# Two attention blocks on one core: the first couple's bounds-check passes over its reciprocals, issued 4 and 6 units later

## The chip, the cores and the metric

The kernel runs on one core of a Trainium2 chip. The metric is the device time of one execution in microseconds; lower is better. Before the change the median of nine runs is 2905.37 us (2904.89 to 2906.02). Tensors are float32 throughout.

## The reference, cut to what matters

Eight samples of 512 channels and 32 x 32 positions pass through two attention layers, each with a residual. The change lies in the first layer, which has 8 heads of 64 channels:

```python
h = group_norm(x, norm_w, norm_b)
qkv = jnp.einsum('oc,bchw->bohw', qkv_w, h) + qkv_b[None, :, None, None]
qkv = qkv.reshape(B, 3, nh, hd, N).transpose(1, 0, 2, 4, 3)
q, k, v = (qkv[0], qkv[1], qkv[2])
attn = jnp.einsum('bhnd,bhmd->bhnm', q, k) * scale
attn = jax.nn.softmax(attn, axis=-1)
o = jnp.einsum('bhnm,bhmd->bhnd', attn, v)
o = o.transpose(0, 1, 3, 2).reshape(B, C, H, W)
o = jnp.einsum('oc,bchw->bohw', proj_w, o) + proj_b[None, :, None, None]
return x + o
```

The second layer is the same with one head of 512 channels and a norm over the whole sample.

## The kernel before, in words

The program is unrolled over the eight samples. For each, `layer0` makes the values, then runs the attention of layer 0, then projects; `attention1` does the second layer. Dense products use a Strassen-like scheme with seven products of quarters in place of eight; that part is away from the change.

**Softmax without a maximum.** The kernel takes exponentials of the raw scores (`exponentials`, L645), multiplies them with the values, and divides the result by the sum of the exponentials. That is right as long as nothing overflows, so the kernel checks bounds: the function `held` (L650 to L654) passes every sum and every reciprocal through ScalarE with the identity function and adds it up along the row into one column of a small tile `extent`. The passed values go to a tile `held` that nobody reads, or, for the sums of a couple, to the tile of the reciprocals-to-be. At the end of the kernel all columns of `extent` are compared with 1e15, and if one is too large, or not a number, a second, slower program with maxima runs. Nothing else reads `extent`.

**Units of attention.** The 8 heads make 4 pairs, taken in the order 0, 2, 1, 3. Each pair has two groups of 512 queries and 8 tiles of keys. One unit is one pair, one group and one tile of keys; 64 units make a sample. The loop at L899 runs over i and issues, in this order: the scores of unit i (L716, TensorE, into a PSUM tile `s`, of which there are two), their exponential (L645, ScalarE) with the sum of exponentials so far (L647, VectorE, `acc`), then the values of unit i - 2 (L735, TensorE, into `ps_o`). When a group of queries is done (after its eighth tile of keys), ScalarE copies one half of `ps_o` out (L741) and VectorE adds the other (L742). Last in each step comes `couple_steps(i)`, in all samples but the eighth, which divides in another way.

**Dividing by couples.** The pairs 0 and 2 make the first couple, 1 and 3 the second. The sums of a couple are finished together, in two parts g = 0 and 1, one for each group of queries. `couple_steps` counts units from the end of the couple's second pair, which for the first couple is unit 31:

- `fold` and `folded` bring together, by DMA and one addition, what the two groups' accumulators hold (1 and 5 steps behind).
- `sum_couple` adds over the partitions by matmuls with ones, into `ps_sum` (7 behind, i = 38).
- `copy_couple` passes part g of the sums through `held` (the bounds check on the sums), out of PSUM into the tile `inv` (7 and 8 behind).
- `one_over_couple` takes the reciprocal of `inv` in place on VectorE (L856) and issues eight DMAs that spread it over the partitions (8 and 10 behind).
- `held_couple` passes the reciprocals through `held` (the bounds check on the reciprocals; L867 to L868). The four numbers in the loop at L888 are the distances of copy, reciprocal, this pass and the division.
- `divide_couple` multiplies the outputs by the spread reciprocals on VectorE (L755; 13 and 15 behind).

The second couple ends with the loop; its steps hang on the q and k products of the next sample (L932 to L945) and go by numbers of their own.

**Order of the work.** The program is written with a manual schedule for TensorE, ScalarE and VectorE: each executes its instructions in the order in which the Python code issues them. The order of DMAs on SyncE is made by a planner. A tile is a buffer from a pool (36 for the large ones, two for `inv`, one for `held`); it comes free after its last reader, and a writer of the next tile in it waits for that.

Of the kernel before, what the change touches and what calls it, by code (L numbers as in the profile page):

```python
# [65 lines left out]
def two_attention_blocks(  # L66
# [31 lines left out]
    def banks(tag, name):  # L98
        return psum.tile([P, 2, HALF], FP, tag=tag, name=name)
# [590 lines left out]
    def layer0(bs, qs, ks, b, norm_next):  # L690
# [133 lines left out]
        def fold(pair):  # L824


            (a, c), t = (accs[pair, g] for g in range(2)), tile2(f"fold_{b}_{pair}")
            low, high = slice(0, HD), slice(HD, P)
            nc.sync.dma_start(t[low], a[high])
            nc.sync.dma_start(t[high], c[low])  # L830
            nc.sync.dma_start(a[high], c[high])
            folds[pair] = t

        def folded(pair):
            a = accs[pair, 0]
            nc.vector.tensor_tensor(a, a, folds.pop(pair), ALU.add)

        def sum_couple(couple, banks_of):


            for n, (pair, j) in enumerate((pair, j) for pair in couple for j in range(2)):
                for g, bank in enumerate(banks_of):
                    rows = slice(g * HD, (g + 1) * HD)
                    nc.tensor.matmul(  # L844
                        bank[n * 32 : (n + 1) * 32, :], ones[rows, :32], accs[pair, 0][rows, j, :],
                        start=True, stop=True,
                    )
            ps_couple[:] = banks_of

        def copy_couple(couple, g):  # L850
            name = f"{b}_{couple[0]}_{g}"
            invs[g] = accpool.tile([P, HALF], FP, tag="inv", name=f"inv_{name}")
            held(ps_couple[g], f"sum_{name}", invs[g])

        def one_over_couple(couple, g):
            nc.vector.reciprocal(invs[g], invs[g])  # L856
            for n, pair in enumerate(couple):
                if g == 0:
                    spreads[pair] = tile2(f"inv_{b}_{pair}")
                for j in range(2):  # L860
                    for r in range(2):
                        nc.sync.dma_start(
                            spreads[pair][(j * 2 + r) * 32 : (j * 2 + r + 1) * 32, g, :],
                            invs[g][(n * 2 + j) * 32 : (n * 2 + j + 1) * 32, :],
                        )

        def held_couple(g):  # L867
            held(invs.pop(g), f"inv_{b}_{g}")  # L868

        def divide_couple(couple, g):  # L870
            for pair in couple:
                divide(pair, g, spreads[pair][:, g, :])

        def ended(i):

            pair, g, kt = units[i] if 0 <= i < len(units) else (None, None, None)
            return pair if (g, kt) == (1, NT - 1) else None

        def couple_steps(i):
            if ended(i - 1) is not None:  # L880
                fold(ended(i - 1))
            if ended(i - 5) is not None:
                folded(ended(i - 5))
            couple = couples[0]
            if ended(i - 7) == couple[1]:
                ps_sum = banks("o", f"ps_sum_{b}_{couple[0]}")
                sum_couple(couple, [ps_sum[:, g, :] for g in range(2)])
            for g, (at_copy, at_over, at_held, at_divide) in enumerate([(7, 8, 10, 13), (8, 10, 12, 15)]):  # L888
                if ended(i - at_copy) == couple[1]:
                    copy_couple(couple, g)  # L890
                if ended(i - at_over) == couple[1]:
                    one_over_couple(couple, g)
                if ended(i - at_held) == couple[1]:
                    held_couple(g)
                if ended(i - at_divide) == couple[1]:
                    divide_couple(couple, g)

        last = norm_next is None
        for i in range(2, len(units) + 2):  # L899
            if i < len(units):  # L900
                score(i)
            values(*units[i - 2], ps.pop(i - 2))
            if not last:
                couple_steps(i)
                continue
            pair, g, kt = units[i - 5] if i >= 5 else (None, None, None)
            name = f"0_{b}_{pair}_{g}"
            if kt == NT - 1 and pair == end:
                ps_sum = banks("o", f"ps_sum_{name}")[:, 0, :]
                add_keys(pair, [g], ps_sum)  # L910
                held(ps_sum, f"sum_{name}")
                invs[pair] = one_over(ps_sum, name)
                divide(pair, g, invs[pair])
            elif kt == NT - 1 and g == 1:
                sum_both(pair, banks("o", f"ps_sum_{name}")[:, 0, :], name)
            pair, g, kt = units[i - 9] if i >= 9 else (None, None, None)
            if pair in invs and kt == NT - 1:
                held(invs.pop(pair), f"inv_0_{b}_{pair}_{g}")
            pair, g, kt = units[i - 10] if i >= 10 else (None, None, None)
            if pair in spreads and (g, kt) == (1, NT - 1):  # L920
                divide_both(pair)
# [809 lines left out]
```

## Time and profile before

| | |
|---|---|
| median of nine runs | 2905.37 us (2904.89 to 2906.02) |
| profiled execution | 2904.69 us, span 2903.0 us, TensorE clock 1.0 |
| TensorE | 2887.8 us busy (99%) |
| VectorE | 1756.5 us (61%) |
| ScalarE | 1090.9 us (38%) |
| `held` over reciprocals or others into the `held` tile (L654) | 41 passes, 630 ns (median) |
| reciprocals of couples (L856) | 28, 3344 ns (median) |
| exponentials (L645) | 512, 1024 ns mean |

The busy times are sums over the one profiled execution. Matmul ends are modelled, so consecutive matmul groups overlap a little in the lists; the distance from start to start is the firmer measure. In a row of waits, the first name is who waited, the second for whom, followed by the total, the number and the longest wait in us. A square bracket at the end of a line of a timeline gives the idle time of the engine just before, and what ended it.

### The profile page before, as it was taken

The numbers are of one execution on the slowest core, as the hardware profiler recorded it, in microseconds if no ns is written. First come the engines' busy times: TensorE is split into PE (matmuls) and PEld (weight loads), VectorE is DVE, ScalarE is ACT, GpSimd is POOL, SyncE is SP. The second block draws the span as 40 slices with busy tenths as digits, with TensorE's granted clock in tenths as the row PEclk, the third lists the DMA queues.
The fourth block names the chain that finished last, engine by engine and source line by source line (L and its number), as shares of the span: only waits on it lengthen the run. The fifth ranks groups of instructions, "written<-read, shape, count | busy, mean of one in ns | idle before, by whom it ended". The sixth has DMA issues, their size and how long they took to land.

```text
span 2903.0 us, 34605 instructions
## 1 busy us (share of the span) xinstructions
PE 2887.8 (99%) x14096; PEld 1363.4 (47%) x14096; DVE 1756.5 (61%) x2196; ACT 1090.9 (38%) x1520; POOL 21.0 (1%) x28
## 2 busy tenths in 40 slices
PE   9999999999999999999999999999999999999999
PEld 6434554345533455335553354533545335453354
DVE  5676366763667536676366753577545775537836
ACT  3462314623155231552315523165222642226431
POOL 0000000000000000000000000000000000000000
PEclk9999999999999999999999999999999999999999
DMA  8412122121222203212032121321212222112001
GB/s 271 158 41 73 51 95 91 41 73 51 94 93 46 84 33 110 79 44 91 26 120 75 41 90 32 113 77 45 83 54 91 77 55 81 54 57 68 8 1 38
DMA packets 77655, 210.79 MB, mean 73 GB/s; under 512 B 19888, under 2 KB 20656, under 8 KB 71088
## 3 DMA queue, kind: packets, MB, share of 16 engines
q1 hardware_dynamic: 77344, 208.48, 22.6%
q8 instruction: 112, 1.84, 0.3%
q14 instruction: 55, 0.45, 0.0%
q10 hardware_dynamic: 144, 0.02, 0.0%
HBM read 137.43 MB, written 28.57 MB: 57 GB/s over the span
## 4 chain that ended last, share of the span: by engine, by line
PE 96%; DVE 3%; ACT 1%; issue 0%; POOL 0%; ACTq 0%; DVEq 0%; POOLq 0%
PE s L716 14%; PE ps_o L735 14%; PE ps_q L479 13%; PE ps_v L494 13%; PE ps_s L1071 13%; PE ps_o L1129 13%; PE ps_k L479 7%; PE ps_p L479 6%; DVE inv L856 2%; DVE acc L647 1%; ACT p L645 1%; PE ps_wvo L596 0%; PE ps_wqk L626 0%; PE ps_o L1140 0%; PE ps_sum L844 0%
## 5 line engine op out<-in xcount | busy, mean ns | idle before, releaser
L645 ACT ACTIVATE p<-s 128x1024 f32<-128x1024 f32 x512 | 521.8, 1024 | 311.4 <-PE s L716 299.9
L716 PE MATMUL s<-q,k 64*64 64x512 f32 x4096 | 531.8, 591 | 8.2 <-ACT p L645 8.2
L647 DVE TENSOR_TENSOR acc<-acc,p 128x1024 f32<-128x1024 f32 x384 | 469.2, 1222 | 107.1 <-ACT p L645 96.7
L735 PE MATMUL ps_o<-p,v 64*64 64x512 f32 x4096 | 528.6, 589 | 0.0
L716 PEld LDWEIGHTS s<-q,k 64*64 64x64 f32 x4096 | 153.2, 133 | 299.4 <-issue 260.3
L735 PEld LDWEIGHTS ps_o<-p,v 64*64 64x64 f32 x4096 | 156.6, 133 | 282.9 <-issue 280.0
L1079 DVE TENSOR_TENSOR p<-ps_s,u_s 128x512 f32<-128x512 f32 x96 | 66.4, 692 | 246.9 <-ACT u_s L421 141.0
L528 DVE TENSOR_TENSOR v<-ps_v,u_v 128x512 f32<-128x512 f32 x96 | 66.2, 690 | 197.5 <-PE ps_v L494 126.2
L421 ACT COPY u_v<-ps_v 128x512 f32<-128x512 f32 x96 | 56.2, 585 | 305.8 <-PE ps_v L494 293.2
L1071 PE MATMUL ps_s<-s_q,t 128*128 128x512 f32 x384 | 167.4, 592 | 0.0
L1129 PE MATMUL ps_o<-t_p,s_v 128*128 128x512 f32 x384 | 166.1, 592 | 0.0
L421 ACT COPY u_q<-ps_q 128x512 f32<-128x512 f32 x96 | 55.8, 581 | 250.4 <-PE ps_q L479 250.4
L647 DVE TENSOR_TENSOR acc<-p,p 128x1024 f32<-128x1024 f32 x64 | 77.9, 1217 | 91.1 <-ACT p L645 91.1
L1081 ACT ACTIVATE p<-p,factor 128x512 f32<-128x512 f32 x96 | 69.3, 722 | 133.2 <-DVE p L1079 133.2
L1071 PEld LDWEIGHTS ps_s<-s_q,t 128*128 128x128 f32 x384 | 73.0, 190 | 91.8 <-issue 91.8
L1129 PEld LDWEIGHTS ps_o<-t_p,s_v 128*128 128x128 f32 x384 | 73.0, 190 | 91.8 <-issue 87.5
L479 PE MATMUL ps_q<-t,w_wqk 128*128 128x512 f32 x256 | 116.0, 597 | 0.0
L479 PE MATMUL ps_p<-t_p,w_p 128*128 128x512 f32 x256 | 114.3, 595 | 0.6 <-DVE inv L658 0.5
L1129 PE MATMUL ps_o<-p,v 128*128 128x512 f32 x256 | 113.3, 595 | 0.0
L494 PE MATMUL ps_v<-w_wvo,t 128*128 128x256 f32 x512 | 113.1, 379 | 0.0
L1071 PE MATMUL ps_s<-q,x 128*128 128x512 f32 x256 | 112.5, 592 | 0.0
L856 DVE RECIPROCAL inv<-inv 128x512 f32<-128x512 f32 x28 | 93.7, 3346 | 22.9 <-ACT inv L654 22.9
(261 smaller groups left out, 3605.8 us busy)
## 6 DMA issues: line engine op xcount, KB each, us to landing
x<-in_x SPq DMA_DIRECT2D x92, 512.0 KB, 7.0
w_qk<-stored_qk SPq DMA_DIRECT2D x14, 1792.0 KB, 7.3
inv<-inv SPq DMA_DIRECT2D x248, 64.0 KB, 2.0
w_wqk<-stored_wqk SPq DMA_DIRECT2D x8, 1792.0 KB, 7.6
fold<-acc SPq DMA_DIRECT2D x56, 256.0 KB, 3.1
w_wvo<-stored_wvo SPq DMA_DIRECT2D x8, 1792.0 KB, 7.8
out<-x SPq DMA_DIRECT2D x28, 512.0 KB, 2.8
w_v<-stored_v SPq DMA_DIRECT2D x7, 1792.0 KB, 7.1
```

The costliest lines, as they stand in the source:

```text
L421: nc.scalar.copy(us[n][:, :width], line[:, :width])
L479: nc.tensor.matmul(bank, w[a][:, k, c * P : (c + 1) * P], bs[b][:, k, :], start=fresh and k == 0, stop=k == 1, skip_group_check=True,)
L494: nc.tensor.matmul(bank[:, u * 2 * P : (u + 1) * 2 * P], bs[b][:, k, n * P : (n + 1) * P], w[a][:, k, :], start=fresh and u == k == 0, sto ...
L645: nc.scalar.activation(p, s, AF.Exp, scale=factor)
L647: nc.vector.tensor_tensor(acc, first, p, ALU.add)
L716: nc.tensor.matmul(s[cols, j, :], flat(ks[pair])[rows, k0 : k0 + HD], qs[pair][rows, g, :], start=True, stop=True,)
L735: nc.tensor.matmul(o[cols, half, :], vs[kt][rows, c0 : c0 + HD], p[rows, j, :], start=kt == 0, stop=kt == NT - 1,)
L856: nc.vector.reciprocal(invs[g], invs[g])
L1071: nc.tensor.matmul(bank, bs[b][:, k, t * P : (t + 1) * P], q_parts[a][:, k, :], start=fresh and k == 0, stop=k == 1, skip_group_check=True,)
L1079: nc.vector.tensor_tensor(p, bank, u, ALU.add)
L1081: nc.scalar.activation(p, bank, AF.Exp, scale=norm.factor)
L1129: nc.tensor.matmul(bank, v_parts[kt // 2][a][:, kt % 2, c * P : (c + 1) * P], p_parts[kt // 2][b][:, kt % 2, cols], start=fresh and kt == ...
```

## The change

In the loop over the two parts of a couple, the third distance, that of `held_couple`, goes from 10 to 14 for g = 0 and from 12 to 18 for g = 1. So the pass over the first part's reciprocals is issued at i = 45 and no longer at i = 41, and that over the second part's at i = 49 and no longer at i = 43. The passes themselves, what they read and what they add into `extent` are the same, and the divisions keep their places (i = 44 and 46), so that both passes now follow them.

```diff
@@ -885,7 +885,7 @@
             if ended(i - 7) == couple[1]:
                 ps_sum = banks("o", f"ps_sum_{b}_{couple[0]}")
                 sum_couple(couple, [ps_sum[:, g, :] for g in range(2)])
-            for g, (at_copy, at_over, at_held, at_divide) in enumerate([(7, 8, 10, 13), (8, 10, 12, 15)]):
+            for g, (at_copy, at_over, at_held, at_divide) in enumerate([(7, 8, 14, 13), (8, 10, 18, 15)]):
                 if ended(i - at_copy) == couple[1]:
                     copy_couple(couple, g)
                 if ended(i - at_over) == couple[1]:
```

## The prediction

> **What bounds the kernel now.** I read the head of the page first, then the whole list of TensorE's waits, which is three rows long.
>
> ```profile
> span 2903.0 us, 34605 instructions
> PE 2887.8 (99%) x14096; PEld 1363.4 (47%) x14096; DVE 1756.5 (61%) x2196; ACT 1090.9 (38%) x1520; POOL 21.0 (1%) x28
> ```
>
> The waits, with their total, number and longest:
>
> ```profile
> PE s L716 <- ACT p L645: 8.2, 7, 1.2
> PE ps_warm L1235 <- POOL in_sample L163: 1.2, 1, 1.2
> PE ps_p L479 <- DVE inv L658: 0.5, 1, 0.5
> ```
>
> TensorE sets the time: it works for 2887.8 of 2903.0 us, and all that it waits for other engines is 9.9 us. Of that, 8.2 us are seven equal stalls of 1.17 us, scores waiting for an exponential. An edit pays or costs here only if it touches those seven stalls or makes new ones. Seven is also the number of samples that run the changed function (all but the last of eight).
>
> Next I read the chain that ended last, around the first stall (start, length, what):
>
> ```profile
> 179.43 3.26 DVE inv L856
> ...
> 184.29 3.35 DVE inv L856
> 187.64 0.02 issue
> 187.66 0.02 ACTq L654
> 187.68 0.04 issue
> 187.72 0.07 ACT held_inv L654
> ...
> 188.26 0.18 ACT held_inv L654
> 188.44 0.92 ACT p L645
> 189.37 0.04 issue
> 189.41 1.09 PE s L716 x8
> ```
>
> At each stall the chain leaves TensorE: the couple's second reciprocal on VectorE ends at 187.64, ScalarE's pass over it (held_inv, L654) starts at 187.72, and only then come an exponential and the scores that need its PSUM bank. The timelines of TensorE and of ScalarE there, start and length in us:
>
> ```profile
> 186.35 1.04 PE L716 MATMUL s<-q,k 64*64 64x512 f32 x8
> 187.21 1.04 PE L735 MATMUL ps_o<-p,v 64*64 64x512 f32 x8
> 189.41 1.09 PE L716 MATMUL s<-q,k 64*64 64x512 f32 x8 [1.17 <-ACT p L645]
> 190.32 1.04 PE L735 MATMUL ps_o<-p,v 64*64 64x512 f32 x8
> 191.18 1.04 PE L716 MATMUL s<-q,k 64*64 64x512 f32 x8
> ```
>
> ```profile
> 182.73 0.63 ACT L654 ACTIVATE held_inv<-inv 128x512 f32<-128x512 f32 x1 [0.64 <-DVE inv L856]
> 187.72 0.63 ACT L654 ACTIVATE held_inv<-inv 128x512 f32<-128x512 f32 x1 [2.45 <-DVE inv L856]
> 195.72 1.02 ACT L645 ACTIVATE p<-s 128x1024 f32<-128x1024 f32 x1 [0.69 <-PE s L716]
> 196.63 0.58 ACT L741 COPY o<-ps_o 128x512 f32<-128x512 f32 x1
> 197.43 1.02 ACT L645 ACTIVATE p<-s 128x1024 f32<-128x1024 f32 x1 [0.22 <-PE s L716]
> ```
>
> An undisturbed unit takes 1.716 us on TensorE (0.86 of scores, 0.86 of values; scores at 184.63 and 186.35). Number the steps of the loop by i. The couple's last unit is 31, its sums are made at i=38 (ps_sum at 174.98), so the scores at 186.35 are unit 45 and those at 189.41 unit 46. The first held pass (written at i=41) waits 0.64 us for its reciprocal and delays only exponential 42, with no loss on TensorE. The second (i=43) waits 2.45 us; exponential 44, whose scores end near 185.5, is stuck behind it until 188.44; scores 46 need the bank that it empties.
>
> **What the Trainium skill says.** "PSUM — Partial Sum Buffer", Engine vs sequencer instructions: the queues of ScalarE and VectorE are strict FIFO. The trace agrees: exponential 44 waits 2.5 us behind a pass that it has nothing to do with. "ScalarE: Activation LUTs", What ACT_TABLE_LOAD costs: an ACTIVATE with immediates takes 186 ns + 0.833 ns per element, 613 ns for 512 as an estimate; the trace shows 630 ns (median of 41), and I use the trace. "Perfetto Trace Analysis", Optimizing Tensor Performance: groups should rotate through PSUM banks so that emptying one overlaps the next group's matmuls. Here s rotates through two buffers, so an exponential may be late only until the scores two units on; the numbers follow.
>
> **The change, part by part.** No instruction is added or removed. Fourteen ScalarE passes (two in each of seven samples, 0.63 us each, with a 0.19 us accumulator read that the next instruction overlaps) are issued later, the first at i=45 in place of 41, the second at 49 in place of 43. They issue no DMA. The DMAs that spread the reciprocals belong to the reciprocal's function and stay where they were, so the queue on SyncE is not passed. Nothing reads the pass's output before the end of the kernel, and the reciprocal's two buffers are next taken after i=65.
>
> *Taken away.* The reciprocals end at 182.69 and 187.64 and don't depend on the passes. At i=45 the first has been done for over 5 us, at i=49 the second for some 8 us, so both waits (0.64 and 2.45 us) become zero. What the stall costs TensorE is more than the 1.17 us on its row, because the first group after it is slower: from scores 45 to scores 47 it is 191.18 - 186.35 = 4.83 us where two units take 3.43. That is 1.40 us. All seven stalls are 1.16 or 1.17 us, with the same starts around them. Sum: 7 x 1.40 = 9.8 us.
>
> *What the passes cost in the new places.* A ScalarE exponential takes 0.92 us to the next start, leaving 1.716 - 0.92 = 0.80 us per unit. At i=45, with the stall gone, exponential 45 runs from about 187.5 to 188.4; the pass then takes until 189.0, and exponential 46 has its scores at about 189.2: nothing is late. At i=49 ScalarE also has the copy of a finished output group (L741). Shown in the clock of the trace before: the copy ends at 197.21, the pass would end at 197.84, so exponential 50 starts 0.41 us late and ends at 198.86. Scores 52, which need its bank, start at 199.76: 0.90 us to spare. The next exponential is on time again. Cost nothing, covered by that 0.90 us; if the cover were gone, each 0.1 us over it would be 0.7 us in the sum of seven.
>
> *What is late next.* VectorE gains nothing. From 179.35 it is busy without a gap until 201.6 (two reciprocals of 3.34, then accumulator sums of 1.22 and divides), and it keeps that clock while TensorE runs 1.40 us ahead. So its backlog against TensorE grows by 1.40 us, and exponentials could meet a buffer whose old reader, an accumulator sum, hasn't run. In the program the exponentials in this stretch take buffers released about seven units earlier: unit 50 takes that of 43, whose sum ends at about 190.1 against a need at about 196.0; unit 52 takes one freed by the last divide at 196.2, needed at about 199.5. Margins 6 and 3.3 us. VectorE then has idle gaps (0.35 us at 201.9, 2.27 us before the sum at 210.56) that swallow the 1.40 us. Nothing on TensorE.
>
> Against the profiled execution the sum is 2903.0 - 9.8 = 2893.2 us of span; that execution took 2904.69 us, 0.7 below the median of nine, 2905.37. Subtracting from the median: **2895.6 us**.
>
> **The rivals.**
> *A, part of the gain only.* The late exponential 50, or a buffer given out in another order now that the reciprocals' tiles are released later, brings a new short stall. For: the copy and the pass meet in one step. Against: 0.90 us of cover. Taking 0.3 to 0.8 us per sample gives 7 x 0.3 to 7 x 0.8 = 2.1 to 5.6 us back, so 2897.7 to 2901.2. Losing just the slow group after the stall (7 x 0.23 = 1.6 us) would give 2897.2.
> *B, the gain is made but not kept.* A transfer that doesn't move with TensorE (inputs, weights) holds up the next stage by the 1.40 us: 2905.4. For: VectorE waits 18.8 us in 12 waits for x. Against: TensorE's list has no row for a transfer, and buffers for loads are released by TensorE, which moves them with it.
> *C, slower.* VectorE's backlog becomes the bound: exponential 52 waits in ScalarE's queue for the buffer of the last divide. It decides once that divide is later by 3.3 us plus the 0.90 of slack, 4.2 us; to cancel the gain it takes 5.6, and with 6.4 us each sample loses 0.8 net: 2905.4 + 5.8 = 2911. For: 22 us of VectorE without a gap. Against: nothing on VectorE is added.
> *D, the change does nothing,* were the wait for the reciprocal not what releases the exponential: 2905.4. The equal 2.45 us in every sample and the chain speak against it.
>
> **How the numbers follow.** The forecast 0.83, A 0.08, B and D together 0.05, C 0.04. A change of 0.2% is 5.8 us, about what a measurement of this kernel can tell from none. The forecast (0.34% faster) is beyond it, and so is the mild half of A: faster 0.87; the rest of A with B and D: same 0.09; slower 0.04. Of the forecast alone, the bounds are 1.17 to 1.45 us per sample: 2895.2 to 2897.2. The range 2894.2 to 2899.5 takes this, 1.0 us below for scatter (the nine runs span 1.1), and the mild half of A.
>
> **What would show it.** Right: TensorE's row for L716 behind L645 gone or under 1 us; the wait of held_inv for L856 down from 25.8 us in 21 waits to about 4.2 in 7 (the second couple's, 25.8 - 7 x 3.09); no L856 in the first couple's stretch of the chain; scores 45, 46, 47 in even steps of 1.72 us; the passes about 188.4 and 195.8 us in the first sample. A: a small row of L716 behind L645 at i=52. C: ScalarE's exponentials waiting for VectorE's L755 or L647 at i=50 to 53. B: a new row on TensorE in the stages after. The prediction fails if the stall at scores 46 stays though both passes are gone from there, for then VectorE held the exponential directly.

## The result, and the profile after

The changed kernel takes 2895.68 us (median of 10 runs, 2894.79 to 2896.84) against 2905.55 us for the kernel before (30 runs). The ratio is 0.9966, 95% interval 0.9959 to 0.9974: 9.9 us or 0.34% faster, where 2895.6 was forecast.

The head of the page and all of TensorE's waits, of the kernel after:

```profile
span 2892.9 us, 34626 instructions
PE 2885.8 (100%) x14096; PEld 1363.9 (47%) x14096; DVE 1756.5 (61%) x2196; ACT 1092.3 (38%) x1520; POOL 21.0 (1%) x28
...
PE ps_warm L1235 <- POOL in_sample L163: 1.2, 1, 1.2
PE ps_p L479 <- DVE inv L658: 0.5, 1, 0.5
```

The row of seven waits of the scores (L716) for exponentials (L645) is gone and nothing stands in its place. The counts of instructions on the three compute engines (TensorE, VectorE, ScalarE) are those of before, and their busy times are within 2.0 us. Nothing became cheaper; a wait went.

ScalarE's wait for the reciprocals, from its list of waits before, then after:

```profile
ACT held_inv L654 <- DVE inv L856: 25.8, 21, 2.4
```

```profile
ACT held_inv L654 <- DVE inv L856: 4.2, 7, 0.6
```

The seven that remain belong to the second couple, which the change doesn't touch.

The same stretch of the first sample as shown of before, first TensorE, then ScalarE (start, length; a square bracket is idle time before the instruction):

```profile
186.00 1.04 PE L716 MATMUL s<-q,k 64*64 64x512 f32 x8
...
187.72 1.04 PE L716 MATMUL s<-q,k 64*64 64x512 f32 x8
188.57 1.04 PE L735 MATMUL ps_o<-p,v 64*64 64x512 f32 x8
189.43 1.04 PE L716 MATMUL s<-q,k 64*64 64x512 f32 x8
```

```profile
187.10 1.03 ACT L645 ACTIVATE p<-s 128x1024 f32<-128x1024 f32 x1 [0.69 <-PE s L716]
188.03 0.62 ACT L654 ACTIVATE held_inv<-inv 128x512 f32<-128x512 f32 x1
...
188.88 1.02 ACT L645 ACTIVATE p<-s 128x1024 f32<-128x1024 f32 x1
...
194.89 0.58 ACT L741 COPY o<-ps_o 128x512 f32<-128x512 f32 x1
195.36 0.65 ACT L654 ACTIVATE held_inv<-inv 128x512 f32<-128x512 f32 x1
195.89 0.20 ACT L654 ACTIVATION_READ_ACCUMULATOR held_inv<-inv 128x1 f32 x1
195.98 1.03 ACT L645 ACTIVATE p<-s 128x1024 f32<-128x1024 f32 x1
197.40 1.03 ACT L645 ACTIVATE p<-s 128x1024 f32<-128x1024 f32 x1 [0.39 <-PE s L716]
```

Scores 45, 46 and 47 (186.00, 187.72, 189.43) stand 1.72 us apart. Both passes follow what is ahead of them on ScalarE with no bracket, that is, without waiting. The first fits the gap to within 0.06 us (exponential 46 starts 1.16 us behind its scores, where 1.10 is usual). The second makes exponential 50 late by 0.29 us (it would start at 195.69, 1.11 us behind its scores at 194.58), and the one after has its gap back, shortened to 0.39 us.

The chain shows what a sample takes now. It passes the first product after the loop (start, length) at these times, first before, then after; the second line is one sample later:

```profile
222.26 3.63 PE ps_q L479 x8
...
579.65 3.63 PE ps_q L479 x8
```

```profile
220.51 3.63 PE ps_q L479 x8
...
576.51 3.63 PE ps_q L479 x8
```

A sample takes 579.65 - 222.26 = 357.39 us before and 576.51 - 220.51 = 356.00 after: 1.39 us less. Seven of these are 9.7 us. The spans of the two profiled executions differ by 10.1 us; the other 0.35 us has nothing to do with the change. It is there from the products of the weights at the start of the program on (a group of L626 starts at 21.89 us before and at 21.54 after), and still there when the couple's sums start (174.98 and 174.63).

### The profile page after: what moved, and what is told of

The parts are those of the page before. It is cut to its first block, busy times and chain, and to the rows that moved or that the text cites. A ratio compares the mean times of both kernels' runs of the same rounds, so it can differ in the third digit from the quotient of the medians.

```text
span 2892.9 us, 34626 instructions
## 1 busy us (share of the span) xinstructions
PE 2885.8 (100%) x14096; PEld 1363.9 (47%) x14096; DVE 1756.5 (61%) x2196; ACT 1092.3 (38%) x1520; POOL 21.0 (1%) x28
## 4 chain that ended last, share of the span: by engine, by line
PE 99%; DVE 0%; ACT 0%; issue 0%; POOL 0%; DVEq 0%; POOLq 0%
PE s L716 15%; PE ps_o L735 15%; PE ps_q L479 13%; PE ps_v L494 13%; PE ps_s L1071 13%; PE ps_o L1129 13%; PE ps_k L479 7%; PE ps_p L479 6%; PE ps_wvo L596 0%; PE ps_wqk L626 0%; PE ps_o L1140 0%; PE ps_sum L844 0%; PE ps_q L844 0%; PE ps_sum L748 0%; PE ps_warm L1235 0%; DVE inv L658 0%
## 5 line engine op out<-in xcount | busy, mean ns | idle before, releaser
L645 ACT ACTIVATE p<-s 128x1024 f32<-128x1024 f32 x512 | 523.9, 1025 | 322.3 <-PE s L716 309.9
L647 DVE TENSOR_TENSOR acc<-acc,p 128x1024 f32<-128x1024 f32 x384 | 469.3, 1222 | 103.8 <-ACT p L645 92.0
L716 PE MATMUL s<-q,k 64*64 64x512 f32 x4096 | 531.5, 590 | 0.0
L716 PEld LDWEIGHTS s<-q,k 64*64 64x64 f32 x4096 | 153.9, 133 | 288.9 <-issue 266.1
L647 DVE TENSOR_TENSOR acc<-p,p 128x1024 f32<-128x1024 f32 x64 | 77.9, 1217 | 84.4 <-ACT p L645 84.4
```

Source lines behind the costliest of these rows:

```text
L645: nc.scalar.activation(p, s, AF.Exp, scale=factor)
L647: nc.vector.tensor_tensor(acc, first, p, ALU.add)
L716: nc.tensor.matmul(s[cols, j, :], flat(ks[pair])[rows, k0 : k0 + HD], qs[pair][rows, g, :], start=True, stop=True,)
```

## The experiments

The kernel before took 2905.58 us on the chip of the first four rows and 2905.59 on that of the last four (medians of 21 runs each). The first four rows are edits of the kernel before, the last four of the kernel after. Where passes are added or left out, the number of columns of `extent` is fitted to it; the diffs below don't show that line.

| run | median, us | ratio to before (95%) | waits of L716 for L645, us |
|---|---|---|---|
| first pass moved alone | 2905.45 | 1.0 (0.9991 to 1.0008) | 7.7 in 7 |
| second pass moved alone | 2895.80 | 0.9965 (0.9952 to 0.9977) | none |
| second pass one step later | 2896.07 | 0.9967 (0.9954 to 0.9979) | none |
| both passes at old places, second reciprocal earlier | 2895.63 | 0.9965 (0.9953 to 0.9978) | none |
| after, without the two passes | 2895.34 | 0.9965 (0.9953 to 0.9978) | none |
| after, one more pass | 2895.52 | 0.9966 (0.9953 to 0.9978) | none |
| after, three more passes | 2905.49 | 1.0 (0.9991 to 1.0009) | 7.9 in 7 |
| after, two more reciprocals | 2895.62 | 0.9966 (0.9954 to 0.9979) | none |

### Which of the two passes

```diff
-            for g, (at_copy, at_over, at_held, at_divide) in enumerate([(7, 8, 10, 13), (8, 10, 12, 15)]):
+            for g, (at_copy, at_over, at_held, at_divide) in enumerate([(7, 8, 14, 13), (8, 10, 12, 15)]):
```

> Only the first part's pass moves (10 to 14); the second stays at 12. Theory (the cost is the second pass's 2.45 us wait for its reciprocal, which holds exponential 44 and through the PSUM bank scores 46): no gain, 2905.5 us, the 1.17 us stalls of L716 behind L645 stay, seven of them. Rival (both passes share the cost, since both waited): about half of the gain, 2900 to 2901 us.

2905.45 us, no gain. ScalarE's and TensorE's rows in the list of waits of this run:

```profile
ACT held_inv L654 <- DVE inv L856: 22.5, 14, 2.6
...
PE s L716 <- ACT p L645: 7.7, 7, 1.1
```

TensorE's seven stalls are there as before. ScalarE's waits for reciprocals fell from 21 to 14, so the first pass's wait did go, and it was worth nothing.

```diff
-            ... [(7, 8, 10, 13), (8, 10, 12, 15)]
+            ... [(7, 8, 10, 13), (8, 10, 18, 15)]
```

> Only the second part's pass moves (12 to 18); the first stays at 10, where it waits 0.64 us for its reciprocal. Theory: the whole gain, 2895.7 us, and no wait of L716 for L645, though the 0.64 us waits of the first pass stay on ScalarE. Rival (both passes share the cost): about half of the gain, 2900 to 2901 us.

2895.80 us, the whole gain. ScalarE still waits 8.7 us in 14 for reciprocals, and none of it reaches TensorE. Half of the edit, the move of the first pass, gains nothing by itself.

### Wait, place, or slack

```diff
-            ... [(7, 8, 10, 13), (8, 10, 12, 15)]
+            ... [(7, 8, 10, 13), (8, 10, 13, 15)]
```

> The second part's pass moves by one step only (12 to 13), the first stays. Its reciprocal isn't ready there yet: the pass still waits, about 0.9 us less the end of exponential 44, and holds exponential 45 until about 0.4 us before scores 47 need its bank. Theory (only lateness beyond the two banks' slack costs): the whole gain, 2895.7 us, with the wait of held_inv for L856 still there at 1 us or so per sample. Rival (any wait of a pass for a reciprocal costs TensorE in proportion): 1.0 to 1.4 of 2.45 us remain, so 4 to 6 us lost again, 2899.5 to 2901.5 us.

2896.07 us: one step is enough. The pass still waits, as ScalarE's timeline of this run shows for the first sample; below it, scores 46 and 47 on TensorE:

```profile
187.10 1.02 ACT L645 ACTIVATE p<-s 128x1024 f32<-128x1024 f32 x1 [0.46 <-PE s L716]
189.08 0.63 ACT L654 ACTIVATE held_inv<-inv 128x512 f32<-128x512 f32 x1 [0.96 <-DVE inv L856]
...
189.71 1.92 ACT L645 ACTIVATE p<-s 128x1024 f32<-128x1024 f32 x2
```

```profile
189.43 1.04 PE L716 MATMUL s<-q,k 64*64 64x512 f32 x8
...
191.14 1.04 PE L716 MATMUL s<-q,k 64*64 64x512 f32 x8
```

It waits 0.96 us with exponential 45 behind it. That exponential starts at 189.71 and takes 0.92 us to the next start; scores 47, which need its bank, start at 191.14, on time. In the kernel before, 2.45 us of waiting cost 1.40 us of TensorE; here 0.96 us cost nothing. What counts is how far the lateness goes beyond what two score banks take up, not that a pass waits.

```diff
-            ... [(7, 8, 10, 13), (8, 10, 12, 15)]
+            ... [(7, 8, 10, 13), (8, 8, 12, 15)]
```

> Both passes stay in their old places (10 and 12), but the second reciprocal is issued two steps earlier, right behind the first (10 to 8). It should end near 186.0 us in the clock of the trace before in place of 187.64, and the pass with it; exponential 44 would end about 187.7, scores 46 need its bank at 188.07. Theory (the wait, not the place of the pass): 2895.7 us, up to 2898 if the 0.36 us to spare are not all there. Rival (the pass's place in ScalarE's order is what costs): 2905.5 us.

2895.63 us with both passes where they were before. The second reciprocal came earlier, and with it the DMAs that spread it, which its function issues; the wait ahead of the second pass fell to 0.72 us:

```profile
183.43 0.63 ACT L654 ACTIVATE held_inv<-inv 128x512 f32<-128x512 f32 x1 [0.65 <-DVE inv L856]
...
186.70 0.63 ACT L654 ACTIVATE held_inv<-inv 128x512 f32<-128x512 f32 x1 [0.72 <-DVE inv L856]
```

So the old place in ScalarE's order wasn't bad in itself. It was bad for being ahead of an exponential while its reciprocal stood behind a sum and an addition (L647 and L742) on VectorE.

### What the passes cost in their new places

```diff
                 if ended(i - at_held) == couple[1]:
-                    held_couple(g)
+                    invs.pop(g)
```

> The kernel after, with the first couple's two passes over the reciprocals left out (and their 14 columns of extent): the bounds check of these reciprocals is not done. Theory (in their new places the passes lie wholly in ScalarE's idle time): 2895.7 us within 1 us. Rival (they still cost TensorE something): up to 14 x 0.63 = 8.8 us less, 2886.9 us.

2895.34 us, 0.3 us below the kernel after (2895.68) with overlapping ranges: nothing to be told apart. Fourteen passes of 0.63 us, 8.8 us of ScalarE's time, cost TensorE nothing that can be seen where they now stand.

```diff
                 if ended(i - at_held) == couple[1]:
+                    for n in range(1 if g else 0):
+                        held(invs[g], f"more_{b}_{g}_{n}")
                     held_couple(g)
```

> The kernel after, with the second part's pass done twice at i=49 (one more 0.63 us pass and one more column of extent per sample). In the trace after, exponential 50 starts 0.29 us late and ends 1.01 us before scores 52. Theory: one more pass makes it 0.92 us late, still inside the slack: 2895.7 us. Rival (no slack left, each 0.63 us shows): 4.4 us more, 2900.1 us.

2895.52 us: one more pass per sample is still covered.

With `range(3 if g else 0)` in the same place:

> The kernel after, with the second part's pass done four times at i=49 (three more passes of 0.63 us each and their columns of extent). Theory (slack 1.01 us): exponential 50 ends 1.89 us later than after, 0.88 us past the start of scores 52; with 0.23 us for the slow first group, 1.1 us per sample, 7.8 us in all: 2903.5 us, and a row of seven waits of L716 for L645 near 0.8 us at i=52. Rival (the slack is larger because the values, not the next scores, wait for the exponential): 2895.7 us.

2905.49 us. The stall came where it was expected, but cost 9.8 us, not 7.8. ScalarE, then TensorE in this run:

```profile
195.73 0.64 ACT L654 ACTIVATE held_more<-inv 128x512 f32<-128x512 f32 x1
...
196.50 0.63 ACT L654 ACTIVATE held_more<-inv 128x512 f32<-128x512 f32 x1
...
197.25 0.63 ACT L654 ACTIVATE held_more<-inv 128x512 f32<-128x512 f32 x1
...
198.00 0.63 ACT L654 ACTIVATE held_inv<-inv 128x512 f32<-128x512 f32 x1
...
198.63 1.92 ACT L645 ACTIVATE p<-s 128x1024 f32<-128x1024 f32 x2
```

```profile
196.67 1.04 PE L716 MATMUL s<-q,k 64*64 64x512 f32 x8
197.53 1.04 PE L735 MATMUL ps_o<-p,v 64*64 64x512 f32 x8
199.69 1.09 PE L716 MATMUL s<-q,k 64*64 64x512 f32 x8 [1.12 <-ACT p L645]
200.60 1.04 PE L735 MATMUL ps_o<-p,v 64*64 64x512 f32 x8
201.46 1.04 PE L716 MATMUL s<-q,k 64*64 64x512 f32 x8
```

The stall is the distance from scores 51 to scores 53, 201.46 - 196.67 = 4.79 us, less the 3.43 us of two units: 1.36 us where the expectation had 1.11. Seven are 9.5 of the 9.8 us. Two terms of the expectation were off, in opposite directions. Here a pass behind a pass takes 0.75 to 0.77 us from start to start, not 0.63, so three more are 2.27 us (195.73 to 198.00), 0.38 more than the 1.89 expected and 1.26 beyond the slack of 1.01. And the 0.23 us added for the slow first group was too much: what comes on top of the exponential's lateness is 0.09 us (0.04 from its end to the scores, 0.05 for the slow group).

Why a pass behind a pass takes longer was not tested. The read of the accumulator (0.19 us) alone can't be the reason. In the kernel after, the two copies of the second couple's sums are such passes back to back as well, and they start 0.59 us apart, the second before the first one's read has ended:

```profile
232.12 0.60 ACT L654 ACTIVATE inv<-ps_q 128x512 f32<-128x512 f32 x1 [5.63 <-PE ps_k L844]
232.61 0.20 ACT L654 ACTIVATION_READ_ACCUMULATOR inv<-ps_q 128x1 f32 x1
232.71 0.59 ACT L654 ACTIVATE inv<-ps_k 128x512 f32<-128x512 f32 x1
```

They write two tiles and read PSUM, where the added passes all write the one `held` buffer and read SBUF. That each of these waits for the buffer of the one ahead would fit, but isn't shown.

That this run lands within 0.1 us of the kernel before is chance: it is the same kind of stall, six units further on.

### VectorE's backlog

```diff
-            nc.vector.reciprocal(invs[g], invs[g])
+            for _ in range(3 if g and couple is couples[0] else 1):
+                nc.vector.reciprocal(invs[g], invs[g])
```

> The kernel after, with the reciprocal of the first couple's second part taken three times in place (6.7 us more on VectorE per sample, 1/(1/(1/x))), so that VectorE's backlog grows by 6.7 us at i=41. In this program the planner gives exponentials 52 and 53 other buffers, and those of the divides go to 54 and 56. Theory (VectorE's backlog is far from being the bound): exponential 50 waits for the sum of unit 43 to about 196.4 us, 0.75 us late, inside the slack: 2895.7 us. Rival C of the prediction (it decides from 4.2 us on): 2.5 to 2.7 us per sample, 17 to 19 us, 2913 to 2915 us.

2895.62 us. The three reciprocals, the sums and the divides behind them on VectorE, and the exponentials 50 to 53 on ScalarE, in this run:

```profile
185.13 10.12 DVE L857 RECIPROCAL inv<-inv 128x512 f32<-128x512 f32 x3
195.17 3.82 DVE L647 TENSOR_TENSOR acc<-acc,p 128x1024 f32<-128x1024 f32 x3
198.90 1.29 DVE L755 TENSOR_TENSOR o<-o,inv 128x512 f32<-128x512 f32 x2
...
202.57 1.29 DVE L755 TENSOR_TENSOR o<-o,inv 128x512 f32<-128x512 f32 x2
```

```profile
197.75 1.02 ACT L645 ACTIVATE p<-s 128x1024 f32<-128x1024 f32 x1 [0.47 <-DVE acc L647]
199.08 1.03 ACT L645 ACTIVATE p<-s 128x1024 f32<-128x1024 f32 x1 [0.30 <-DVE acc L647]
200.32 1.02 ACT L645 ACTIVATE p<-s 128x1024 f32<-128x1024 f32 x1 [0.20 <-PE s L716]
202.03 1.02 ACT L645 ACTIVATE p<-s 128x1024 f32<-128x1024 f32 x1 [0.69 <-PE s L716]
```

The exponentials 50 and 51 do begin to wait for VectorE's sums, 0.47 and 0.30 us, and the slack takes it up. What rival C describes doesn't come about in this program: exponentials 52 and 53 start at 200.32 and 202.03, before the last two divides are done (from 202.57 to 203.86), so neither of them takes a buffer that these divides free. At which backlog VectorE does become the bound wasn't tried; in this program 6.7 us are not enough.

## Why the prediction was right

- **What the stall cost.** 7 x 1.40 = 9.8 us was forecast; 1.39 us per sample and 9.9 us between the medians were measured. That the forecast time is met within 0.1 us is closer than the executions agree among themselves (they span 2 us), and so in part luck; the cost per sample is the firmer test. The forecast took the distance from scores to scores, not the row of waits (8.2 us). That choice was right, but one reason given for it was mostly wrong. Of the 0.23 us by which the 1.40 exceeds the 1.17 on the row, only 0.05 is the slow group after the stall (0.91 us to the next start where 0.86 is usual). The other 0.18 is the modelled end of the matmul group ahead, which lasts 1.04 us on the list though the next group usually starts after 0.86: the wait is counted only from that end.
- **Which pass.** The prediction gave the first pass's wait no loss on TensorE and the second all of it. The two passes moved alone show just that: 2905.45 and 2895.80 us.
- **Nothing in the new places.** Forecast: exponential 50 late by 0.41 us with 0.90 us to spare. Measured: 0.29 us late, and its end at 197.01 is 1.01 us ahead of scores 52 at 198.02. The pass starts a little before the copy ahead of it ends, hence the difference. One more pass is free there, three more are not.
- **What is late next.** VectorE kept its own times, as forecast: its second reciprocal starts at 183.94 after and at 184.29 before, the same once the 0.35 us of the start are taken off. ScalarE's list after has no wait of an exponential for a sum of L647.
- **The rivals.** A (a new short stall), B (the gain given back in a later stage) and D (no effect) didn't happen: TensorE's list has no row for them, and the gain of 1.39 us stands from one sample to the next. C (VectorE as the bound) stays untested at its price. It was put 4.2 us of lateness away, for an exponential that takes the buffer of the last divide; the run with 6.7 us had other buffers there (by its expectation those of the divides go to units 54 and 56), so it neither confirms nor refutes that limit. In C's sum the last step should read 7 x 0.8 = 5.6 and not 5.8, which leaves its 2911 as it is.

## What to carry to other kernels

An instruction whose result nobody needs until the end can still set the time, if it waits at the head of an in-order queue ahead of one that is needed. Look in the chain for such a waiter, and issue it after its input is sure to be there, in a step with idle time on its engine. Price the stall by the distance between equal pieces of work across it, and work out the slack that the buffers give: waits within it, here 0.64 and 0.96 us, cost nothing, and so moving them gains nothing.

## What the runs showed of the hardware

An identity pass with an accumulated sum on 128 x 512 takes 0.63 us of ScalarE ahead of an exponential, which starts before the pass's accumulator read (0.19 us) has ended. Ahead of another such pass it takes 0.59 us where the two read PSUM and write tiles of their own, and 0.75 to 0.77 us where both read SBUF and write the same buffer. Which of the two differences counts is open.
